# Two graph layers with experts: layer 1's adjacency product by pairs of panels in seven block products, and scores of three tiles in four by TensorE

## The chip, the cores and the metric

The kernel runs on one core of one Trainium2 chip. The core has a matrix engine (TensorE, PE in the profile; its weight loads are shown as PEld), a vector engine (VectorE, DVE), a scalar engine (ScalarE, ACT), a general engine (GpSimd, POOL) and a queue engine that issues transfers (SyncE, SP). They run side by side, each takes its own instructions in order, and they wait for one another by semaphores. The metric is the time of one execution on the device in microseconds (us), as the median over runs.

## The reference

Two layers work on 3327 nodes with 256 features each, in fp32. Each layer adds a graph step to `x`, and then a mixture of experts:

```
# layer 0
x = x + relu(adj @ (LN(x) @ W) + b)
x = x + moe0(LN(x))                        # 8 experts, 256 -> 1024 -> 256, best two of 8 per node
# layer 1
sim  = tanh(adj * adj);  filt = sim * (adj > 0)     # the 700 largest per row are kept
h2   = tanh(LN(x) @ W_proj + b_proj)
x = x + relu(filt @ (h2 @ W_gcn) + b_gcn)
t = LN(x)
x = x + t + sum over the best two experts of  p * (gelu(t @ w1[e] + b1[e]) @ w2[e] + b2[e])
```

`adj` is 3327 x 3327 with a few nonzero elements per row, but it is multiplied as a dense matrix. No row has more than 700 nonzero elements with these inputs, so the selection of the 700 largest leaves all of them; the kernel tests this and has another branch for the other case.

## The kernel before, in words

Nodes are padded to 3328, which is 26 tiles of 128 nodes, or 13 panels of 256 nodes. `x` and the features `s` (one row per node: `h2 @ W_gcn` in layer 1) stay in SBUF, with nodes on the partitions. The host hands over the transposed adjacency cut into 26 pieces: a panel (256 result nodes) by half of the source nodes (13 slices of 128). A piece is 1.7 MB. Six places in SBUF (`ring`, the constant `RING`) hold pieces; the tables `LOADS` and `ENDS`, made from `UNITS`, say in which order pieces are loaded and given up, and so which piece goes to which place.

Layer 0 aggregates its panels 2 to 11 by pairs (`pair` in `aggregate_first`). Two panels by two halves of the source nodes are a 2 x 2 block matrix, and the two halves of the source nodes by two halves of the features are another. The scheme of Strassen and Winograd gets their product from seven block products where the plain way has eight. It needs sums of blocks: four sums of whole pieces per pair (`add_pieces`, line 480, on VectorE, in place, each in four parts) and, once, four sums of feature blocks (`sum_features`, kept in `pad` as `half_sums`). There the features are the stationary operand and the piece, 256 columns wide, is the moving one, so that the results lie with features on the partitions (line 470), and a product with `W` turns them.

Layer 1's aggregation is `aggregate` (lines 430 to 450). For each panel it runs 52 matmuls (two halves, two result tiles, 13 slices): the piece gives the stationary 128 x 128 operand, `s[:, j, :]` with all 256 features is the moving one, and results lie with nodes on the partitions, as `x` does. Then `add_relu` (lines 403 and 404) adds bias, relu and residual. `filter_chunk` (lines 1656 to 1661) turns a loaded piece into `tanh(max(a, 0)^2)` in place: the maximum on VectorE, Square and Tanh on ScalarE. The first four pieces are filtered by `filter_behind` while the features are still being made.

`after1` (lines 1683 to 1695) does the routing behind each panel. It lists the tokens of the panel before (`list_tokens`: two small bf16 matmuls per tile, lines 770 and 771, give each token its place in the list of its expert, and GpSimd scatters each token twice, line 793). Then it normalizes the two tiles (`statistics`, then line 371 on VectorE) and scores them: `scores` (line 662) is eight multiply-and-sum instructions per tile on VectorE, one for each expert. The last panel's tiles are scored by TensorE instead (`by_features` turns the tiles by `transpose`, `scores_by_product` multiplies, line 672). `weights` picks the two best experts (`top_two`), takes the exponential on ScalarE (line 729) and makes the shares. GpSimd adds the normalized tokens to `x` (line 1690) and copies them for the second expert (line 765). At panel 9 `plan_early` makes, from the tokens of panels 0 to 8, a table of eight full blocks of 256 tokens, and at panels 10 and 11 the first four of these blocks, with their experts' weights, are loaded into free places of the ring.

After the last panel (`first_blocks`) the expert blocks run one after the other; the last panel's routing and the plan of all other blocks come between the first three of them.

The order of the instructions on each engine is made at build time. A scheduler walks through the program with a model of the times and takes, for each engine, the first instruction in program order that its model holds to be ready; the engine then keeps that order on the chip. `issue_after` and `behind` force an instruction behind another one on the same engine.

## Time and profile before

| | |
|---|---|
| median of 4 runs | 1202.94 us (1200.27 to 1203.8) |
| the profiled execution: its own time | 1199.63 us |
| the profiled execution: span from first to last instruction | 1197.8 us |
| mean granted TensorE clock | 0.987 |
| layer 1's aggregation | 750.5 to 1045.9 us of the span |
| in it: TensorE, VectorE, ScalarE, GpSimd busy | 295.4, 243.6, 154.9, 72.9 us |
| from there to the end | 151.9 us, TensorE busy 121.9 |

How to read the lines: a line of a view names the engine, the line of the kernel (L440), the operation, what is written and read (`ps_g<-s,ring`), the shapes, and how many instructions are merged (x104). In the views in order of time a line begins with start and duration in us. In brackets stands the idle time of the engine before the instruction, and what ended it. A matmul in fp32 leaves two records, and so does its weight load. Matmuls are pipelined: the duration of one is longer than the distance from one to the next, and the distance is what a series costs. A line can be that of a helper: L793 is every scatter, L480 every sum of pieces.

### The profile page before, as it was taken

To read this page: it belongs to the slowest core of one execution; us is meant where nothing else is said; L and a number is where in the kernel's file an instruction comes from. 1 tells how busy PE (TensorE), PEld (TensorE's weight loads), DVE (VectorE), ACT (ScalarE), POOL (GpSimd) and SP (SyncE) were. 2 spreads that over 40 slices of the span, in tenths; PEclk is the share of its full clock that TensorE was granted. 3 is DMA by queue.
4 is the path that set the end of the run, shared out by engine and by line. 5 is a ranking of instruction groups with operands and counts; after the bars stand their busy time and mean duration, and the time that the engine had idled before them with its cause. 6 is when DMAs were issued, how large, how long until landed. Compare 5 with 4: busy or idle time off the path is not lost. (4 is left out here: it accounts for less than half of the span.)

```text
span 1197.8 us, 19704 instructions
## 1 busy us (share of the span) xinstructions
PE 1156.5 (97%) x6217; PEld 1006.7 (84%) x6217; DVE 865.8 (72%) x3001; ACT 556.9 (46%) x1051; POOL 291.6 (24%) x367
## 2 busy tenths in 40 slices
PE   8999999999899999999999999999999999989983
PEld 7888888888688888898988888888888888877862
DVE  6798999988865555554545679299999998784464
ACT  5599566541224333434334346976546542033331
POOL 2111242143421112111111110022232232265442
PEclk9999999999999999999999999999999999999997
DMA  9895747634366555757565964245445442467697
GB/s 348 192 325 187 255 144 210 246 126 144 110 232 230 197 185 191 264 181 264 190 232 171 368 239 166 97 150 189 165 174 189 155 184 75 131 205 234 209 291 226
DMA packets 123185, 241.68 MB, mean 202 GB/s; under 512 B 24480, under 2 KB 93120, under 8 KB 116160
## 3 DMA queue, kind: packets, MB, share of 16 engines
q1 hardware_dynamic: 108656, 205.59, 51.7%
q0 software_dynamic: 11136, 31.60, 7.1%
q10 hardware_dynamic: 3280, 3.15, 0.8%
q8 instruction: 51, 0.84, 0.3%
q14 instruction: 62, 0.51, 0.1%
HBM read 203.98 MB, written 36.33 MB: 201 GB/s over the span
## 5 line engine op out<-in xcount | busy, mean ns | idle before, releaser
L440 PE MATMUL ps_g<-s,ring 128*128 128x256 f32 x1352 | 294.2, 380 | 0.0
L440 PEld LDWEIGHTS ps_g<-s,ring 128*128 128x128 f32 x1352 | 256.0, 190 | 34.4
L1234 ACT ACTIVATE pad<-ps_h,ring 128x256 f32<-128x256 f32 (+1 forms) x282 | 128.8, 458 | 296.7 <-issue 143.9
L1226 PE MATMUL ps_h<-pad,ring 128*128 128x256 f32 (+1 forms) x1184 | 254.5, 367 | 5.0 <-issue 2.6
L1226 PEld LDWEIGHTS ps_h<-pad,ring 128*128 128x128 f32 x1184 | 200.5, 190 | 47.9 <-ACT pad L1234 10.5
L662 DVE SCALAR_TENSOR_TENSOR rt_product<-xn,gate 128x256 f32<-128x256 f32 x400 | 194.8, 487 | 16.1 <-ACT xn L360 2.8
L793 POOL DMA_INDIRECT ys<-pad,index x114 | 116.4, 1021 | 369.6 <-DVE pad L1281 236.1
L793 POOL DMA_INDIRECT xlist<-xn,rt_idx x104 | 115.4, 1110 | 157.1 <-DVE ln_nw L347 60.8
L1495 ACT ACTIVATE sign<-ring,below 128x416 bf16<-128x416 f32 x208 | 133.4, 641 | 11.8 <-DMA ring<-in_adjT 5.9
L470 PE MATMUL ps_g<-ring,pad 128*128 128x256 f32 x520 | 115.0, 380 | 0.0
L470 PEld LDWEIGHTS ps_g<-ring,pad 128*128 128x128 f32 x520 | 98.5, 190 | 13.2
L1660 ACT ACTIVATE ring<-ring 128x3328 f32<-128x3328 f32 x22 | 65.4, 2978 | 87.3 <-DVE ring L1659 56.3
L1281 DVE SCALAR_TENSOR_TENSOR pad<-ps_y,ring,pad 128x128 f32<-128x128 f32 x176 | 59.2, 348 | 47.6 <-PE ps_y L1274 47.4
L470 PE MATMUL ps_g<-ring,s 128*128 128x256 f32 x390 | 89.6, 379 | 0.0
L470 PEld LDWEIGHTS ps_g<-ring,s 128*128 128x128 f32 x390 | 74.1, 190 | 10.1
L480 DVE TENSOR_TENSOR ring<-ring,ring 128x768 f32<-128x768 f32 (+1 forms) x80 | 79.6, 1013 | 0.0
L495 PE MATMUL ps_g<-ring,s 128*128 128x256 f32 x312 | 69.1, 380 | 3.5 <-ACT s L360 3.0
L495 PEld LDWEIGHTS ps_g<-ring,s 128*128 128x128 f32 x312 | 58.9, 190 | 12.7 <-ACT s L360 3.7
L1661 ACT ACTIVATE ring<-ring 128x3328 f32<-128x3328 f32 x22 | 65.4, 2978 | 0.6
L1265 DVE TENSOR_TENSOR xnT<-pad 128x512 f32<-128x512 f32 x22 | 15.2, 692 | 59.2 <-ACT pad L1234 59.2
L1323 PE MATMUL ps_y<-ring,pad 128*128 128x256 f32 x224 | 56.3, 399 | 0.0
L776 POOL COPY xn<-rt_w 128x4 f32<-128x4 f32 x26 | 4.8, 198 | 201.0 <-DVE rt_w L738 200.9
(240 smaller groups left out, 1587.7 us busy)
## 6 DMA issues: line engine op xcount, KB each, us to landing
ring<-in_adjT SPq DMA_DIRECT2D x50, 1664.0 KB
ring<-in_f_w1T SPq DMA_DIRECT2D x30, 1024.0 KB
ring<-in_f_w2T SPq DMA_DIRECT2D x30, 1024.0 KB
ring<-xlist SPq DMA_DIRECT2D x52, 258.0 KB
ring<-in_f_w SPq DMA_DIRECT2D x36, 256.0 KB
ring<-ys SPq DMA_DIRECT2D x12, 512.0 KB
ring<-in_f_b SPq DMA_DIRECT2D x34, 128.0 KB
xlist<-h2T SPq DMA_DIRECT2D x16, 257.0 KB
```

Source lines behind the costliest of these rows:

```text
L440: nc.tensor.matmul(ps[it], lhsT=chunks[k][:, c, ts(it, P)], rhs=s[:, j, :], start=(j == 0), stop=(j == NT - 1),)
L470: nc.tensor.matmul(ps, lhsT=b[:, c, :], rhs=a[:, c, :], start=(first and c == 0), stop=(c == CJ - 1), skip_group_check=not first,)
L480: nc.vector.tensor_tensor(out[:, part, :], out[:, part, :], other[:, part, :], ALU.add)
L495: nc.tensor.matmul(sums[pan][c], lhsT=s[:, j, ts(c, P)], rhs=piece(pan, j // CJ)[:, j % CJ, :], start=(j == 0), stop=(j == NT - 1),)
L662: nc.vector.scalar_tensor_tensor(product, xn, 1.0, gate[:, e, :], ALU.mult, ALU.mult, accum_out=sc[:, g, e : e + 1],)
L793: d = nc.gpsimd.indirect_dma_start(out=a[:, :], out_offset=bass.IndirectOffsetOnAxis(ap=index, axis=0), in_=rows_, in_offset=None,)
L1226: last_product[:] = [nc.tensor.matmul(ps, lhsT=w1[:, c, ts(hc, P)], rhs=xT[:, c, :], start=(c == 0), stop=(c == DC - 1),)]
L1234: nc.scalar.activation(hT[:, hc, :], ps, func, bias=bb1[:, hc : hc + 1])
L1281: last_y[:] = [nc.vector.scalar_tensor_tensor(part, ps, xb[:, g, WT : WT + 1], part, ALU.mult, ALU.add)]
L1495: nc.scalar.activation(sign, piece(pan, k)[:, :, ts(i, GROUP)], AF.Sign, bias=below, accum_out=positive[:, pan, i, k : k + 1],)
L1660: nc.scalar.activation(a, a, AF.Square)
L1661: nc.scalar.activation(a, a, AF.Tanh)
```

## The change

Layer 1's panels are cut into units: panel 0 alone, the pairs (1,2), (3,4), (5,6), (7,8) and (9,10), and panels 11 and 12 alone. A pair is done in seven block products with the same sums as in layer 0, but the piece stays the stationary operand and the half block of features (128 columns) is the moving one, so that results lie with nodes on the partitions. Each product is 13 slices by two result tiles; the PSUM results are copied by ScalarE into `g1` and `g2` or added to them by VectorE, and `add_sums` adds bias, relu and residual for a whole panel.

The routing of a unit is cut into named steps (`route1`), which run at fixed places within the next unit, as hooks within a product or between products. Normalization moves to ScalarE (`scaled`). Of the four tiles of a pair, three are scored by TensorE and one by VectorE where another pair follows, and two by each where panel 11 follows (`BY_PRODUCT`). Panel 0's two tiles are scored by TensorE, panel 11's two by VectorE. Of the four pieces that are filtered in a pair, two have their maximum taken by VectorE and two by a Relu on ScalarE. The passes of ScalarE over a piece are put between its other work (`run`, `passes`), each behind the last copy. `shares` moves from `weights` into `list_tokens`. The early plan is made from the same panels 0 to 8, but within the last product of the pair (9,10); the four early blocks are loaded as places come free from then on.

```diff
+BY_PRODUCT = {(1, 2): 2, (2, 2): 3, (2, 1): 2, (1, 1): 0}
 UNITS = (
     [(pan,) for pan in range(SIDE)] + [(pan, pan + 1) for pan in range(SIDE, NPAN - 1, 2)] + [(NPAN - 1,)],
-    [(pan,) for pan in range(NPAN)],
+    [(0,)] + [(pan, pan + 1) for pan in range(1, NPAN - 2, 2)] + [(NPAN - 2,), (NPAN - 1,)],
 )
...
-    def aggregate(b_sb, prepare, after):
...
+    def aggregate(b_sb, route, freed, turn, copied):
...
+        def filter_next(on_vector):
+            if not loaded_:
+                return
+            a = piece(*loaded_.pop(0)).rearrange("p c w -> p (c w)")
+            if on_vector:
+                with behind(normal):
+                    nc.vector.tensor_scalar(a, a, 0.0, None, ALU.max)
+            for f in ([] if on_vector else [AF.Relu]) + [AF.Square, AF.Tanh]:
+                passes.append((a, f))
+
+        def run(n):
+            for a, f in passes[0:n]:
+                with behind(copied):
+                    last_pass[:] = [nc.scalar.activation(a, a, f)]
+            del passes[0:n]
...
+        def multiply(ps, a, b, first=True, hooks=()):
+            hooks = dict(hooks)
+            ps = by_tile(ps)
+            for c in range(CJ):
+                for it in range(PW // P):
+                    nc.tensor.matmul(
+                        ps[:, it, :], lhsT=a[:, c, ts(it, P)], rhs=b[:, c, :],
+                        start=(first and c == 0 and it == 0), stop=(c == CJ - 1),
+                        skip_group_check=True,
+                    )
+                if c in hooks:
+                    hooks[c]()
...
+        def add_sums(pan, g):
+            x_t = x[:, pan * 2 : pan * 2 + 2, :]
+            nc.vector.tensor_tensor(g, g, b_tiles, ALU.add)
+            nc.vector.scalar_tensor_tensor(x_t, g, 0.0, x_t, ALU.max, ALU.add)
+
+        def pair(p1, p2, step, ps_x, ps_q, ps_b, ps_z):
+            a11, a12, a21, a22 = (piece(pan, k) for pan in (p1, p2) for k in range(NCHUNK))
+            b11, b21, b22 = half(0, 0), half(1, 0), half(1, 1)
+            t3, t2, t4, t1 = half_sums
+            run(len(passes))
+            multiply(ps_x, a11, b11)
+            (g1, (c11, c12)), (g2, (c21, c22)) = sums_of(), sums_of()
+            copy(c11, ps_x)
+            step("statistics")
+            with behind(last_shift):
+                add_pieces(a11, a21)
+            add_pieces(a21, a22)
+            filter_next(False)
+            run(2)
+            multiply(ps_q, a22, t4)
+            copy(c21, ps_q)
+            run(1)
+            filter_next(True)
+            step("normalized")
+            add_pieces(a22, a11)
+            run(1)
+            multiply(ps_b, a12, b21)
+            nc.vector.tensor_tensor(c11, c11, by_tile(ps_b), ALU.add)
+            add_pieces(a12, a22)
+            step("other scores")
+            turn_ = lambda: step("turned")
+            multiply(ps_z, a21, t1, hooks={2: turn_, 7: turn_})
+            run(1)
+            copy(c22, ps_z)
+            free(p2, 0)
+            score = lambda: step("scores")
+            multiply(ps_x, a22, t2, False, {2: score, 6: score})
+            step("weights")
+            copy(c12, ps_x)
+            free(p2, 1)
+            filter_next(False)
+            run(1)
+            step("exponentials")
+            run(2)
+            multiply(ps_z, a12, b22, False)
+            free(p1, 1)
+            nc.vector.tensor_tensor(c12, c12, by_tile(ps_z), ALU.add)
+            add_sums(p1, g1)
+            multiply(ps_x, a11, t3, False, {2: lambda: step("listed"), 8: lambda: step("planned")})
+            filter_next(True)
+            for part in (c21, c22):
+                nc.vector.scalar_tensor_tensor(
+                    part, part, -1.0, by_tile(ps_x), ALU.mult, ALU.subtract
+                )
+            add_sums(p2, g2)
+            free(p1, 0)
...
+                hooks = {
+                    0: lambda: step("statistics", "normalized"),
+                    2: lambda: step("other scores"),
+                    16: lambda: step("turned"),
+                    18: lambda: step("turned"),
+                    28: lambda: step("scores"),
+                    30: lambda: step("scores", "weights", "exponentials"),
+                    42: lambda: step("listed"),
+                    48: lambda: step("planned"),
+                }
+                if turn and u[0] == NPAN - 1:
+                    hooks[22] = turn
+                single(u[0], hooks, banks[0:2])
...
-        if group == "0":
-            w = shares(w, n)
+        w = shares(w, n)
...
-    def panels1(layer1, turn=False):
...
+    def route1(pans, by_product, ready, copied):
...
+        def normalize():
+            for at in range(0, n, 2):
+                xn = work.tile([P, 2, K, RW], F32, name="xn")
+                for g in range(2):
+                    copied.append(scaled(xn[:, g, 0, 0:D], t + at + g, at + g, q.rs, q.shift))
+                x_t = x[:, t + at : t + at + 2, :]
+                nc.gpsimd.tensor_tensor(x_t, x_t, xn[:, :, 0, 0:D], ALU.add)
+                q.xns.append(xn)
+            q.sc = work.tile([P, n, E], F32, name="rt_sc", bufs=2)
...
+        def turn_(i):
+            q.xnTs.append(turned_tiles(tiles_at(i), "xnT"))
+            copied.append(last_turned[0])
+
+        def score(i):
+            m = len(tiles_at(i))
+            scores_by_product(q.xnTs[i], m, f1_r_sb, q.sc[:, 2 * i : 2 * i + m, :])
+
+        def score_rest():
+            for g in range(by_product, n):
+                score_tile(q.xns[g // 2][:, g % 2, 0, 0:D], q.sc[:, g, :])
...
+        def plan_():
+            if pans[-1] + 1 == EARLY_PANS[1]:
+                plan_early(EARLY_PANS[1])
+            if pans[-1] + 1 >= EARLY_PANS[1]:
+                ready()
...
-        aggregate(gnn_b_sb, filter_chunk, panels1(layer1, True))
+        aggregate1(layer1, layer1.turn_first)
```

## The prediction

> **What bounds the kernel now.** I read the busy time by engine first, then the windows of layer 1's aggregation, then the matmuls by shape, then the instructions in order of time.
>
> ```profile
> PE 1156.5 (97%) x6217; PEld 1006.7 (84%) x6217; DVE 865.8 (72%) x3001; ACT 556.9 (46%) x1051; POOL 291.6 (24%) x367
> ```
> ```profile
> 750.50:1045.90 295.40, 295.40 (x1410) 259.24 (x1409) 243.63 (x924) 154.94 (x86) 72.86 (x91) 1.00 0.43 150
> 1045.90:1197.80 151.90, 121.87 (x624) 100.01 (x622) 86.99 (x331) 48.14 (x99) 67.56 (x69) 0.92 0.74 235
> ```
> The columns of a window are: length, then busy time of PE, PEld, DVE, ACT, POOL, then granted clock, DMA share, GB/s. The stage that is changed lasts from 750.5 to 1045.9 us, and TensorE has no gap in it at full clock (1.00). So only TensorE's own work, or a wait that is new to it, moves the end of this stage. What follows (151.9 us) hangs on the end of panel 12 in both kernels.
>
> ```profile
> 796.44 0.17 PE L770 MATMUL pr<-rt_both,before 128*128 128x8 bf16 x1
> ...
> 796.54 22.69 PE L440 MATMUL ps_g<-s,ring 128*128 128x256 f32 x104
> 819.07 0.17 PE L770 MATMUL pr<-rt_both,before 128*128 128x8 bf16 x1
> ```
> A panel lasts from one listing to the next: 819.07 - 796.44 = 22.63 us; four small listing matmuls take 0.10 of it, so 104 records of 256 columns take 22.53 us, 0.2166 us each. (An fp32 matmul leaves two records, so 52 matmuls are 104.)
>
> ```profile
> 402.25 0.97 PEld L1274 LDWEIGHTS ps_y<-gate,pad 128*128 128x128 f32 x8
> 403.14 0.97 PEld L1274 LDWEIGHTS ps_y<-ring,pad 128*128 128x128 f32 x8
> 404.03 1.87 PEld L1274 LDWEIGHTS ps_y<-gate,xnT 128*128 128x128 f32 x16
> 405.82 0.97 PEld L1274 LDWEIGHTS ps_y<-ring,h2T 128*128 128x128 f32 x8
> ```
> This is layer 0's expert in seven products: the shape that the change brings in (128 weights, 128 moving columns). From 402.25 to 405.82, 32 records: 0.1116 us each. The load's own duration is 0.192 us, but loads start 0.112 us apart, so the spacing and not the duration counts.
>
> ```profile
> 194.30:237.30 43.00, 43.00 (x212) 37.79 (x209) 40.28 (x134) 26.74 (x73) 12.57 (x14) 1.00 0.68 219
> ```
> One pair of panels in layer 0, already done in seven products: TensorE busy for all of 43.0 us although VectorE works for 40.28.
>
> **The change, part by part.**
>
> *Products.* Ten of thirteen panels go by pairs. Removed: 10 x 22.53 = 225.3 us. Added per pair: 7 products x 13 slices x 2 halves of the panel x 2 records = 364 records of 128 columns, x 0.1116 = 40.6 us; five pairs 203.1. Panels 0, 11 and 12 stay as they are. Saved: 22.2 us, all of it on the engine that sets the end. One eighth would be 28; six go because a record of half the columns costs 0.1116 instead of 0.1083.
>
> A rule stands against this. The Trainium skill (TensorE: Matmul & The Clock Gate, "LDWEIGHTS (loading the stationary operand)" and "The mechanism") prices a load at its columns over 1.2 GHz, 107 ns here, and says that loads overlap matmuls in flight only where the row group differs. With full 128-row loads that adds about 0.107 to each record; by this estimate a pair would take some 79 us and the change would lose about 170. The row above was taken with exactly these shapes and shows 0.1116 for load and matmul together, so the sum goes by the row.
>
> *Scores by TensorE.* Tiles scored so: two of panel 0, three of four in the pairs (1,2) to (7,8), two of (9,10): 2 + 12 + 2 = 16. A tile needs two transposes and four records of scores.
>
> ```profile
> 400.93 0.46 PEld L1172 LDWEIGHTS ptb<-ident,ring 128*128 128x128 f32 x4
> 401.35 0.97 PEld L1274 LDWEIGHTS ps_y<-ring,pad 128*128 128x128 f32 x8
> ...
> 1055.08 0.97 PEld L672 LDWEIGHTS pg<-f_r_sb,xnT 128*128 128x128 f32 x8 [0.21 <-ACT xnT L388]
> 1055.97 0.73 PEld L1226 LDWEIGHTS ps_h<-pad,ring 128*128 128x128 f32 x4
> ```
> Four transposes take 401.35 - 400.93 = 0.42, eight score records 0.89. A tile: 0.21 + 0.45 = 0.66 us, and 16 tiles 10.5 us, in the middle of TensorE's row. Nothing covers it there. The eight-column output does not help, since its loads are full.
>
> *VectorE per pair,* from layer 0's 40.3 us: three tiles fewer of scores (32 of them with their reads took 14.3 + 2.6, so -12.7); two filter passes (2 x 1.88 = +3.8; the other two pieces go to ScalarE); bias and relu on two panels as four instructions of 0.68 instead of eight of 0.42 (-0.7); the output sums nearly as before (+0.2); two score copies (+0.3); layer 0's bias on the scores goes (-0.2). Sum 31.0. To this comes GpSimd's x + xn, which layer 0 lacks:
>
> ```profile
> 849.06 2.06 DVE L662 SCALAR_TENSOR_TENSOR rt_product<-xn,gate 128x256 f32<-128x256 f32 x1
> ...
> 849.54 1.28 POOL L1690 TENSOR_TENSOR x<-x,xn 128x512 f32<-128x512 f32 x1
> ```
> A VectorE instruction of 0.42 took 2.06 while it ran. Two of these per pair: +2.6, so 33.6 of a pair's 42.9 us (40.6 + 2.0 for three tiles + 0.3 for eight listing records). VectorE does not become the bound by its sum.
>
> The sums of the weights (four instructions of 1.88) run once, in panel 0, in which VectorE was busy for 3 of 22.6 us: no cost.
>
> *ScalarE per pair:* Square and Tanh on four pieces and Relu on two, 10 x 2.98 = 29.8; four normalizations of 0.59; four PSUM copies of 0.37; two copies of turned tiles, 0.59 + 0.37; one Exp of 0.20: 34.9 of 42.9. No table load: the trace has four in all, and Relu, Identity, Exp, Square and Tanh alternate elsewhere without one.
>
> *Waits, walked through a pair,* t from its first product; products end near 5.8, 11.6, 17.4, 23.9 (with transposes), 30.9 (with scores), 36.7, 42.8. On VectorE the last pair's two sums, relu and residual end at 2.2, its statistics and shift, a chain of some 13 small steps of 0.2 each, at 6.3; the first two panel sums (3.98 each, from four parts of 1.21 and 0.95) at 14.3: product 4 starts at 17.4, slack 3.1. A filter pass (1.9), the third sum and the 2.6 of GpSimd give 22.8: product 5 starts at 23.9, slack 1.1. The fourth sum ends at 27.2 against 30.9. On ScalarE a Relu, Square and Tanh stand ahead of the normalizations, which end near 17.7; the first transposes come at 18.3, slack 0.6. Thus no stall by the rows, but two slacks near one microsecond. Bounds: 0 from layer 0's pair, which had none with more on VectorE; from above, every sum at its slowest part (1.23 x 4) and all 4.2 us of GpSimd's sums and copies falling on them: 6.3 + 3 x 4.9 + 1.9 + 4.2 = 27.1, product 5 waits 3.2 per pair, 16 in all. I take 0 in the pairs, as the nearest row does.
>
> *Panel 11* has the whole routing of pair (9,10) in 22.6 us with two tiles scored by VectorE (2 x 4.2), after the early plan (some 27 small steps, about 6 us, moved from panel 9's end to this pair's last product). Plan, sums and statistics reach to about 10, scores to 20, weights to 23, while the listing is written at 18. TensorE may wait there: between 0 and 5, taken as 1.5. The expert loads queue on SyncE behind the last pieces, not ahead, and wait for scatters that land near 10 us into panel 11; the first is used 20 us later: no cost.
>
> *Piece loads.* Two pieces issued together at 841.94 were through by 852, so one is there about 7 us after its issue; freed at 23.9 and 30.9, needed at 42.8 or later after two or three passes: hidden. The order of the first six pieces changes, and the first pair needs its fourth piece 11.6 us after panel 0, at 784.8; before, the sixth piece's Tanh ended near 785.2. 0 to 0.5, taken as 0.
>
> *After the stage:* panel 11's list is made inside panel 12 instead of behind it. That frees 5 us of GpSimd's queue, on which TensorE doesn't wait. 0.
>
> Sum: -22.2 + 10.5 + 1.5 = -10.2 us. The profiled execution took 1199.63 us (span 1197.8 and 1.8 around it) and would take 1189.4. The median of the runs shown, 1202.94, lies 3.3 above it, so the forecast is 1192.7.
>
> **Rivals.**
>
> 1. *Slower:* product 5 waits for the third panel sum in every pair. For it: VectorE's window is filled in layer 0 to 40.28 of 43.0, GpSimd's lock is real (2.06 for 0.42), slack is 1.1. Against it: layer 0's pair, busier, has no gap. It cancels the gain at 10.2 / 5 = 2.0 us per pair; at the upper bound of 3.2 it costs 16: 1208.7. The Trainium skill (SBUF — State Buffer, "SBUF: two separate sides") calls the shared port an exclusive lock when a VectorE instruction has two SBUF inputs, as the panel sums have. The row of 2.06 agrees; by the page too it is GpSimd's own time that VectorE can lose.
> 2. *Partial:* ScalarE's row runs late (normalizations behind three passes, a piece that lands late), and transposes or listings stand in TensorE's queue for about 1 us per pair, panel 11 for 5: +3.5 to +9, 1196 to 1202.
> 3. *Better:* transposes and scores slip into the gaps between products, or the products' loads overlap better than in short runs. With half of the 10.5 gone and no wait in panel 11: -17, 1186.
> 4. *The change doesn't do what it says:* a record of 128 columns costs the load's whole 0.192 in a long run. A pair would take 70 + 2.3 us, 135 more in all, 1338. The 56 records in a row at 0.112 speak against it; 1%.
>
> **How the numbers follow.** Forecast 66%, with its own range 1188 to 1198; partial 14%; slower 14%; better 5%; the last 1%. Runs of this kernel can tell about 0.2% (2.4 us) from no change. Below 1200.5: the forecast, the better case and half of the partial one, 78%; within 0.2%: 7%; above 1205.3: 15%. Range 1184 to 1207: down to a better case, up to half-way into the slower one.
>
> **What would show it.** Right: the pairs' matmuls 0.112 us apart and a pair in 43 us; the stage ends near 1036 instead of 1045.9; VectorE about 34 of 43 per pair. Wrong: idle TensorE before products 4 or 5 released by VectorE's panel sums, before transposes released by ScalarE's normalizations, or before panel 11's listing; a spacing above 0.12.

## The result, and the profile after

The changed kernel takes 1200.07 us (median of 52 runs, 1194.34 to 1207.89) beside 1201.37 us of the kernel before (78 runs). The ratio is 0.9985, with a 95% interval from 0.9977 to 0.9993: some 1.8 us less, which is within the 0.2% that I took as no change. The forecast was 1192.7 us. The profiled execution took 1199.55 us with a span of 1197.8 us, the same span as before.

The busy time by engine, after:

```profile
PE 1145.7 (96%) x7093; PEld 1022.3 (85%) x7093; DVE 851.6 (71%) x2667; ACT 603.5 (50%) x1110; POOL 313.0 (26%) x367
```

TensorE works 10.8 us less than before (1156.5), close to the sum of the terms *Products* and *Scores by TensorE* (-22.2 + 10.5 = -11.7). The work went, and the time stayed. The windows of the stage and of what follows, and then of the stage's units (the five pairs, panel 11, panel 12), show where; the columns are length, busy time of PE, PEld, DVE, ACT, POOL, then granted clock, DMA share, GB/s:

```profile
748.30:1044.60 296.30, 289.07 (x2287) 277.77 (x2286) 227.28 (x594) 202.16 (x145) 94.98 (x93) 0.99 0.44 154
1044.60:1197.80 153.20, 121.83 (x620) 100.12 (x618) 87.65 (x327) 48.02 (x99) 64.94 (x68) 0.92 0.71 226
```
```profile
771.60:813.76 42.16, 42.16 (x381) 42.14 (x380) 29.46 (x63) 36.19 (x20) 8.69 (x4) 1.00 0.45 162
813.76:856.69 42.93, 42.93 (x392) 42.92 (x391) 37.64 (x86) 33.78 (x22) 11.86 (x13) 1.00 0.49 174
856.69:899.62 42.93, 42.93 (x393) 42.92 (x391) 37.92 (x86) 33.14 (x22) 16.89 (x16) 1.00 0.52 184
899.62:944.23 44.61, 44.31 (x393) 43.36 (x392) 37.73 (x86) 33.16 (x22) 16.35 (x16) 1.00 0.51 178
944.23:988.66 44.43, 44.16 (x393) 43.46 (x392) 38.24 (x92) 33.37 (x22) 17.04 (x17) 1.00 0.40 140
988.66:1018.80 30.14, 23.47 (x114) 19.77 (x113) 20.61 (x95) 5.86 (x8) 12.05 (x14) 0.89 0.42 128
1018.80:1044.57 25.77, 25.77 (x129) 22.64 (x127) 18.37 (x80) 3.36 (x6) 12.07 (x16) 1.00 0.42 139
```

Before, TensorE had no gap in this stage; now the stage has 7.2 us of gaps (296.30 - 289.07) and a clock below 1.00. The second and third pair take 42.93 us, where the prediction said 42.9. The fourth and fifth take 1.7 and 1.5 us more. Panel 11 takes 30.14 us for 23.47 of work, part of it at a low clock. The stage as a whole takes 296.3 us where 285 were forecast. That it starts 2.4 us earlier than before (748.3 against 750.7) and is followed by 1.3 us more (153.2 against 151.9) makes the spans equal.

The products, in order of time (a line has the start, the duration, the operation and, after the x, the records that are merged):

```profile
813.76 5.97 PE L679 MATMUL ps_g<-s,ring 128*128 128x128 f32 x52
819.57 5.97 PE L679 MATMUL ps_g<-pad,ring 128*128 128x128 f32 x52
825.38 5.97 PE L679 MATMUL ps_g<-s,ring 128*128 128x128 f32 x52
```

From start to start 5.81 us for 52 records: 0.1117 us each, against 0.1116 forecast. The estimate that the prediction drew from the Trainium skill (TensorE: Matmul & The Clock Gate, "LDWEIGHTS (loading the stationary operand)" and "The mechanism"), by which each full 128-row load would add about 0.107 us, is not what this shape does on the chip. The second of these sections also names loads into a background weight buffer as pulled ahead of matmuls in flight; the prediction's estimate left that case out.

Panel 11, in order of time, is where it went wrong:

```profile
988.66 9.66 PE L753 MATMUL ps_g<-s,ring 128*128 128x256 f32 x44
1004.25 1.18 PE L388 MATMUL pt<-ident,xn 128*128 128x128 f32 x4 [5.93 <-ACT xn L361]
1005.23 4.22 PE L753 MATMUL ps_g<-s,ring 128*128 128x256 f32 x14
...
1017.98 0.18 PE L923 MATMUL pr<-rt_both,before 128*128 128x8 bf16 x1 [0.74 <-DVE rt_both L854]
```

The four transposes of pair (9,10)'s tokens wait 5.93 us for ScalarE's normalization, and stand in TensorE's queue ahead of panel 11's own matmuls. ScalarE has nothing to do before it; it waits for VectorE's `ln_shift`. And this is VectorE in the middle of the Newton steps (small steps that approximate one over a square root) that lead to it:

```profile
997.10 0.16 DVE L348 SCALAR_TENSOR_TENSOR ln_nw<-ln_guess 128x4 f32<-128x4 f32 x1
1002.89 0.17 DVE L1397 CAST index<-ring 128x2 int32<-128x2 f32 x1 [5.63 <-DMA ring<-xlist]
1002.97 0.15 DVE L349 TENSOR_TENSOR ln_nw<-ln_nw,ln_ve 128x4 f32<-128x4 f32 x1
```

An instruction that belongs to another stage stands between two steps of 0.2 us and waits 5.63 us for a transfer. It is in `place_of` (line 1397): the conversion of the first expert block's token numbers into whole numbers. The block's first work on TensorE comes 29 us later (1031.42), in panel 12. Its input is the block's tokens, and their load waits for the scatters of panels 7 and 8 (first the last scatter on GpSimd's queue, then the load on SyncE's):

```profile
997.31 0.97 POOL L945 DMA_INDIRECT xlist<-xn,rt_idx  x1 [0.30 <-issue]
```
```profile
1000.05 0.40 SPq L1288 DMA_DIRECT2D ring<-xlist  x1
```

In the kernel before, the same conversion stood later and waited for 0.81 us, and TensorE ran through:

```profile
1012.54 0.17 DVE L1245 CAST index<-ring 128x2 int32<-128x2 f32 x1 [0.81 <-DMA ring<-xlist]
```

The change moved the early plan from panel 9's end to the last product of pair (9,10), and the build-time scheduler puts each instruction where its model holds it to be ready; here the load came later than the place that it chose.

The wait has a second price. Windows of the same columns, around the gap:

```profile
998.00:1004.20 6.20, 0.32 (x2) 0.00 (x0) 0.55 (x4) 0.60 (x2) 0.66 (x3) 0.70 0.49 145
1004.20:1006.20 2.00, 1.95 (x7) 1.57 (x8) 0.99 (x1) 1.94 (x4) 1.43 (x2) 0.50 0.61 145
1006.20:1008.20 2.00, 2.00 (x8) 1.65 (x7) 1.93 (x5) 0.00 (x0) 2.00 (x3) 0.72 0.80 246
1008.20:1017.90 9.70, 9.04 (x46) 7.74 (x44) 9.23 (x40) 0.00 (x0) 0.75 (x1) 1.00 0.44 128
```

After the gap the granted clock is 0.50 for 2 us and 0.72 on average over 2 more. From the first of the four transposes to the next record it takes 0.98 us instead of 0.44, and the next 14 records take 4.05 us (1005.23 to 1009.28) instead of the 3.03 that 14 x 0.2166 gives: about 1.6 us together.

Panel 11 from the listing that opens it (983.80) to its own (1017.98) took 34.2 us. Its work is 40 records of 128 columns (4.5), 90 of 256 (19.5), four transposes (0.4), eight scores (0.8) and 0.2 of small matmuls: 25.4, counted by distances. The excess of 8.8 us is 5.93 + 0.74 of waits, about 1.6 of slow clock and some 0.5 around the two waits.

The rest of the loss is in the fourth and fifth pair. The weight loads of their second product, in order of time:

```profile
905.32 2.73 PEld L679 LDWEIGHTS ps_g<-pad,ring 128*128 128x128 f32 x22
908.36 0.52 PEld L679 LDWEIGHTS ps_g<-pad,ring 128*128 128x128 f32 x4 [0.31 <-issue]
909.11 1.28 PEld L679 LDWEIGHTS ps_g<-pad,ring 128*128 128x128 f32 x9 [0.22 <-issue]
910.59 0.52 PEld L679 LDWEIGHTS ps_g<-pad,ring 128*128 128x128 f32 x4 [0.20 <-issue]
```

They stop for 0.2 to 0.3 us every few records, and "issue" says that the profile shows nothing that they wait for. The product lasts 7.65 us instead of 5.97.

### The profile page after: what moved, and what is told of

The parts are those of the page before. It is cut to its first block, busy times and chain, and to the rows that moved or that the text cites. A ratio compares the mean times of both kernels' runs of the same rounds, so it can differ in the third digit from the quotient of the medians.

```text
span 1197.8 us, 21265 instructions
## 1 busy us (share of the span) xinstructions
PE 1145.7 (96%) x7093; PEld 1022.3 (85%) x7093; DVE 851.6 (71%) x2667; ACT 603.5 (50%) x1110; POOL 313.0 (26%) x367
## 5 line engine op out<-in xcount | busy, mean ns | idle before, releaser
L1378 PEld LDWEIGHTS ps_h<-pad,ring 128*128 128x128 f32 x1184 | 200.9, 190 | 48.3 <-ACT pad L1386 10.5
L459 DVE TENSOR_TENSOR ring<-ring,ring 128x768 f32<-128x768 f32 (+1 forms) x160 | 168.9, 1096 | 1.7 <-PE ps_g L679 1.7
L660 ACT ACTIVATE ring<-ring 128x3328 f32<-128x3328 f32 x54 | 160.1, 2979 | 0.8 <-DMA ring<-in_adjT 0.4
L945 POOL DMA_INDIRECT xlist<-xn,rt_idx x104 | 118.8, 1142 | 126.2 <-DVE rt_idx L934 51.7
L1647 ACT ACTIVATE sign<-ring,below 128x416 bf16<-128x416 f32 x208 | 133.4, 641 | 13.5 <-DMA ring<-in_adjT 7.5
L818 DVE SCALAR_TENSOR_TENSOR rt_product<-xn,gate 128x256 f32<-128x256 f32 x272 | 122.4, 450 | 15.6 <-ACT xn L361 6.0
L679 PE MATMUL ps_g<-pad,ring 128*128 128x128 f32 x1040 | 126.0, 277 | 0.6
L679 PEld LDWEIGHTS ps_g<-pad,ring 128*128 128x128 f32 x1040 | 120.1, 192 | 2.2 <-issue 1.7
L679 PE MATMUL ps_g<-s,ring 128*128 128x128 f32 x780 | 89.6, 275 | 0.0
L679 PEld LDWEIGHTS ps_g<-s,ring 128*128 128x128 f32 x780 | 88.4, 192 | 0.1
L753 PE MATMUL ps_g<-s,ring 128*128 128x256 f32 x312 | 70.0, 384 | 0.0
L753 PEld LDWEIGHTS ps_g<-s,ring 128*128 128x128 f32 x312 | 59.6, 193 | 8.0
```

The costliest lines, as they stand in the source:

```text
L459: nc.vector.tensor_tensor(out[:, part, :], out[:, part, :], other[:, part, :], ALU.add)
L660: last_pass[:] = [nc.scalar.activation(a, a, f)]
L679: nc.tensor.matmul(ps[:, it, :], lhsT=a[:, c, ts(it, P)], rhs=b[:, c, :], start=(first and c == 0 and it == 0), stop=(c == CJ - 1), skip_g ...
L753: nc.tensor.matmul(banks_[it], lhsT=piece(pan, k)[:, c, ts(it, P)], rhs=s[:, j, :], start=(j == 0), stop=(j == NT - 1),)
L818: nc.vector.scalar_tensor_tensor(product, xn, 1.0, gate[:, e, :], ALU.mult, ALU.mult, accum_out=sc[:, e : e + 1],)
L945: d = nc.gpsimd.indirect_dma_start(out=a[:, :], out_offset=bass.IndirectOffsetOnAxis(ap=index, axis=0), in_=rows_, in_offset=None,)
```

## The experiments

Kernels of one group ran on the same chip and share the runs of the kernel before there. Different groups ran on different chips or at different times, and the kernel before itself had medians from 1188.41 to 1207.75 us in them. So each is given as a ratio to the kernel before of its own group, with its 95% interval. "Stage" is the length of layer 1's aggregation in the trace, from its first matmul to the end of panel 12 (295.3 us before, 296.3 after).

| group | kernel | ratio to before | stage, us |
|---|---|---|---|
| 1 | `cast_behind` | 0.9942 [0.9921, 0.9963] | 287.9 |
| 1 | `cast_all_product` | 0.9935 [0.9910, 0.9960] | 289.8 |
| 1 | `cast_no_product` | 1.0120 [1.0093, 1.0146] | 305.0 |
| 1 | `before_scores` | 1.0208 [1.0174, 1.0243] | 318.2 |
| 2 | `after_again` | 0.9984 [0.9967, 1.0001] | 297.0 |
| 2 | `cast_behind_again` | 0.9936 [0.9916, 0.9955] | 291.2 |
| 2 | `cast_listing` | 0.9932 [0.9912, 0.9952] | 288.5 |
| 2 | `cast_two_listing` | 0.9948 [0.9931, 0.9964] | 292.9 |
| 3 | `after_third` | 1.0060 [1.0026, 1.0094] | 297.7 |
| 3 | `phase` | 1.0040 [1.0009, 1.0070] | 297.3 |
| 4 | `before_again` | 0.9987 [0.9967, 1.0007] | 295.2 |
| 4 | `cast_listing_again` | 0.9987 [0.9966, 1.0009] | 295.1 |
| 5 | `listing_control` | 0.9940 [0.9917, 0.9963] | 291.5 |
| 5 | `listing_shift80` | 0.9940 [0.9919, 0.9961] | 293.2 |
| 5 | `listing_shift160` | 0.9938 [0.9919, 0.9956] | 291.2 |

### The conversion at the head of VectorE's queue

One instruction of the changed kernel is moved: the conversion must stand behind the last bias-and-relu of panel 12. In the traces of the two kernels the order of the instructions on TensorE, VectorE, ScalarE and GpSimd differs in this one alone.

```diff
@@ add_relu
-        nc.vector.scalar_tensor_tensor(x_tile, t, 0.0, x_tile, ALU.max, ALU.add)
+        last_added[:] = [nc.vector.scalar_tensor_tensor(x_tile, t, 0.0, x_tile, ALU.max, ALU.add)]
@@ place_of
-            with behind(last_y):
+            with behind(last_y), behind(last_added if group == "1" else ()):
```

Expected of `cast_behind`:

> The changed kernel with one instruction moved: the conversion of the first expert block's token numbers (index<-ring), which in the changed kernel stands on VectorE in the middle of the statistics of pair (9,10), is forced behind the last bias-and-relu of panel 12; nothing else moves on any engine. Theory A (VectorE's queue was held by that one instruction, which waited 5.63 us for the load of the first expert block): the statistics end near 998 instead of 1003.4, the transposes of panel 11 wait about 1 us instead of 5.93, TensorE's clock is not halved behind the gap, and the program is 6 to 7 us shorter than the changed kernel, 0.993 of the kernel before. Rival B (VectorE is simply too full there, with the early plan, the sums and the statistics of four tiles in one stretch): the transposes wait as long as before, and the time changes by less than 1 us, 0.998 to 0.999. Rival C (the wait comes back before the listing of panel 11, which waits for the best two experts from VectorE): half of the gain, 0.996.

Panel 11 in its trace, in order of time:

```profile
983.72 9.66 PE L753 MATMUL ps_g<-s,ring 128*128 128x256 f32 x44
993.67 0.93 PE L388 MATMUL pt<-ident,xn 128*128 128x128 f32 x4 [0.30 <-ACT xn L361]
994.44 3.19 PE L753 MATMUL ps_g<-s,ring 128*128 128x256 f32 x14
...
1007.75 0.18 PE L923 MATMUL pr<-rt_both,before 128*128 128x8 bf16 x1 [2.32 <-DVE rt_both L854]
```

The transposes wait 0.30 us instead of 5.93, and the 14 records behind them run at full speed (3.19 us instead of 4.22). Panel 11 goes from listing to listing in 28.9 us instead of 34.2. Part of what is gained is given back at the listing, which now waits 2.32 us instead of 0.74. The ratio is 0.9942.

Since chips differ, the changed kernel and this one ran once more, side by side.

Expected of `after_again`:

> The changed kernel, unchanged, beside the kernel before on the same chip as the three below. Theory A (the held VectorE queue costs panel 11 some 5 us, and cast_behind gains by letting it go): 0.9985 of the kernel before, as measured over several chips, and cast_behind_again 4 to 5 us less than this run. Rival B (the chip of the first four runs was kinder to the changed kernel, and moving the conversion gained nothing): this run gives 0.994 to 0.995 itself, within 1 us of cast_behind_again.

Expected of `cast_behind_again`:

> The conversion of the first expert block's index behind panel 12's last bias and relu, once more, now beside the changed kernel itself. Theory A: 0.994 of the kernel before, and 0.9955 of the changed kernel (-5 us), with pairs of 42.9 us and transposes in panel 11 that wait under 0.5 us. Rival B: equal to after_again within 1 us.

The changed kernel gave 0.9984 again, with its transposes waiting 6.24 us and a stage of 297.0; the moved conversion gave 0.9936 and 291.2. By the medians (1198.83 and 1194.98 us) one instruction's place costs 3.9 us. The stages differ by 5.8, but not all of that is the instruction's: 5.4 us are gained in panel 11 (34.8 and 29.4 from listing to listing), 1.6 are lost in panel 12 to a clock that was halved behind the listing's wait of 2.23 us, and 2.1 are gaps in the fourth and fifth pair that this trace has less of (their part follows below). Theory A holds, and the rival that only the chip differed is out.

### What the scores by TensorE are worth

`before_scores` is the kernel before with the tiles of panels 0 to 11 scored by TensorE, and nothing else:

```diff
-        sc = scores(xns, n) if pan < NPAN - 1 else scores_by_product(by_features(xns[0], n), n, f1_r_sb)
+        sc = scores_by_product(by_features(xns[0], n), n, f1_r_sb)
```

Expected of `before_scores`:

> The kernel before, with one part of the change alone: the 24 tiles of panels 0 to 11 are scored by TensorE (two transposes, four score records a tile) where VectorE did it; panels stay single. Theory A (nothing covers these on a TensorE without gaps): 24 x 0.66 = 15.8 us longer, 1.013 of the kernel before. Rival (they slip between the products): less than 4 us longer, below 1.003.

It lost 23.5 us (1211.86 against 1188.41), 1.0 us for each of its 24 tiles and not 0.66, so the rival that they slip between the products is out. The waits of TensorE's weight loads in its aggregation (what was waited for, us in total, times, longest):

```profile
PEld pt L387 <- issue: 4.9, 9, 0.6
PEld pg L672 <- ACT xnT L388: 2.3, 11, 0.2
PEld pt L387 <- DVE xn L371: 1.7, 8, 0.5
PEld pt L387 <- PE ps_g L440: 1.6, 2, 1.0
```

These are 10.5 us of waits around transposes and scores. The tiles' own 15.8 and these waits make 26, a little more than was lost.

The other half, the products alone, is `cast_no_product`: the moved conversion, and no tile of panels 0 to 11 scored by TensorE. `cast_all_product` goes the other way, with every tile.

```diff
-BY_PRODUCT = {(1, 2): 2, (2, 2): 3, (2, 1): 2, (1, 1): 0}
+BY_PRODUCT = {(1, 2): 0, (2, 2): 0, (2, 1): 0, (1, 1): 0}     # cast_no_product
+BY_PRODUCT = {(1, 2): 2, (2, 2): 4, (2, 1): 4, (1, 1): 2}     # cast_all_product
```

Expected of `cast_no_product`:

> As cast_behind, but all tiles of layer 1's panels 0 to 11 are scored by VectorE, none by TensorE: the block products alone. If the prediction's sum for TensorE is right, its row gets 16 x 0.66 = 10.5 us shorter; but VectorE, busy 37.7 of 42.9 us in a pair of the changed kernel, gets three tiles more, 12.7 us, or 50.4 against 40.9 on TensorE. Theory A: VectorE becomes the bound of four pairs, each about 50 us, and panel 11 takes about 6 us more: some 35 us longer than cast_behind, near 1.022 of the kernel before. Rival (VectorE's work is hidden, its waits do not matter): 10 us shorter than cast_behind, 0.985.

Expected of `cast_all_product`:

> As cast_behind, but every tile of panels 0 to 11 is scored by TensorE: eight tiles more than in the change. Theory A (once the held queue is gone, TensorE's row alone sets the time): 8 x 0.66 = 5.3 us longer than cast_behind, 0.997 to 0.998 of the kernel before, less what is left of the wait before panel 11's listing, which goes since VectorE has 8 us less to do there. Rival B (VectorE is too full): as fast as cast_behind or faster, 0.99.

Without TensorE's scores the change loses: 1.0120. Windows of its second and third pair:

```profile
805.70:857.30 51.60, 46.35 (x418) 46.16 (x415) 48.86 (x127) 38.46 (x21) 11.36 (x10) 0.99 0.59 208
857.30:907.20 49.90, 47.00 (x398) 46.62 (x398) 47.12 (x138) 36.41 (x21) 18.90 (x16) 0.94 0.45 159
```

VectorE is busy for 47 to 49 us of these pairs, which TensorE would do in 41 (42.93 - 3 x 0.66), and TensorE stands at the listing, 18.6 us in five waits for `rt_both` in the whole stage. VectorE is the bound there. It took 19.4 us more than `cast_behind` (1202.19 against 1182.75), where Theory A had 35: two of the four pairs took about 50 us, the other two 47.9 and 46.7, and panels 11 and 12 took no more than there. With every tile by TensorE, the window of a pair, and below it the like pair of `cast_behind`:

```profile
851.30:894.80 43.50, 43.50 (x398) 43.50 (x396) 34.51 (x71) 33.27 (x22) 17.06 (x16) 1.00 0.52 182
```
```profile
850.08:893.00 42.92, 42.92 (x392) 42.91 (x390) 37.81 (x87) 33.14 (x22) 17.12 (x16) 1.00 0.53 185
```

From listing to listing such a pair takes 43.59 us (851.30 to 894.89) against 42.92: a tile costs TensorE 0.67 us and frees 3.3 us of VectorE. Its eight more tiles cost 8 x 0.67 = 5.4 us, and the waits of 0.30 and 2.32 us in panel 11 are gone. In the traces its stage is 1.8 us longer than that of `cast_behind`; the ratios, 0.9935 and 0.9942, don't tell the two apart. That TensorE's row sets the pairs is as Theory A has it, and the time is nearer to Rival B's.

### Where VectorE's tiles stand in the way

Expected of `cast_listing` (the moved conversion, all tiles of pair (9,10) and of panel 11 by TensorE, three of four in the other pairs: `(2, 2): 3, (2, 1): 4, (1, 1): 2`):

> With the conversion behind; all four tiles of pair (9,10) scored by TensorE instead of two, and both tiles of panel 11 instead of none. Theory A (in panel 11 VectorE's two scored tiles, 8.4 us, make the listing late by 2.7 us, and as much in panel 12): four tiles cost TensorE 4 x 0.6 = 2.4 us and the two waits of 2.7 and 3.1 go: -3.4 us against cast_behind_again, 0.991 of the kernel before. Rival B (the listing is late for another reason, such as the statistics): the waits stay and the tiles cost 2.4 us: 0.996.

Expected of `cast_two_listing` (the same with `(2, 2): 2`):

> As cast_listing, and two tiles instead of three in the pairs followed by a pair. TensorE's pair goes from 42.9 to 42.3 us, VectorE's from 37.9 to 41.3 us of it. Theory A (TensorE sets the pair until VectorE's sum reaches it): -0.6 x 4 = -2.4 us against cast_listing, 0.989 of the kernel before. Rival B (VectorE's chain from panel sums to the listing is already the bound at 41.3, as with no tile by TensorE, where pairs took 46.7 to 51.6): the listing waits 0.5 to 2 us per pair, so 0 to +6 us against cast_listing, 0.991 to 0.996.

In this trace of `cast_listing` neither the transposes nor the listing of panel 11 wait; it goes from 983.84 to 1010.15, 26.3 us, beside 34.8 in `after_again` and 29.4 in `cast_behind_again`. (In the four later traces of this kernel and its shifted variants the transposes do wait, for 1.2 to 2.0 us, and the panel takes 27.6 to 28.4.) The ratio is 0.9932. The gain on `cast_behind_again` is 2.7 us by the stages and 1.75 by the medians, where 3.4 was expected; the intervals are too wide to tell these apart. In `cast_two_listing` a pair takes 42.26 us with VectorE busy for 40.6 of it, as Theory A has it, and no listing waits but the fifth pair's, 0.6 us. But by the medians it was 3.5 us slower than `cast_listing` (1196.70 against 1193.23), by the stages 4.4, and the trace shows what neither theory named:

```profile
987.77 9.23 PE L753 MATMUL ps_g<-s,ring 128*128 128x256 f32 x42
1000.59 0.69 PE L388 MATMUL pt<-ident,xn 128*128 128x128 f32 x2 [3.58 <-issue]
```
```profile
989.89 1.89 DVE L653 TENSOR_SCALAR ring<-ring 128x3328 f32<-128x3328 f32 x1 [2.42 <-DMA ring<-in_adjT]
```

Here a filter pass of a late piece (line 653) stood at the head of VectorE's queue for 2.4 us, the early plan and the statistics came behind it, and the transposes waited 3.6 us. It looks like the same fault with another instruction, one that waits for a transfer and holds VectorE's chain behind it. But the same pass waits 0.99 us in `cast_listing` too, and VectorE came to it 5.1 us after the listing here and 2.3 us after it there; no run moved this pass alone, so its share in the 3.6 us is not shown.

### The gaps in product 2

These gaps without a wait were the open part. The first thought was that TensorE's instructions come late. The profile's table of DMA queues has two marked "instruction"; one of them (q8) moved 58 packets of together 0.95 MB, so 16 KB each, and 51 in the kernel before, which has fewer instructions on TensorE. By narrow windows one of these packets starts every 14 us or so of a pair and takes about 1 us, and in products 2 of pairs 2 to 5 one starts 12 to 14 us after the listing that opens the pair. The gaps lie at 13 to 17 us. `phase` makes the stream of TensorE 80 instructions longer at its start, in a gap:

```diff
-WARM = 54
+WARM = 94
```

Expected of `after_third` (the changed kernel again, as the neighbour):

> The changed kernel, unchanged, as the neighbour of the run below on the same chip. 0.9985 of the kernel before. In both traces so far the weight loads of the second product of the fourth and fifth pair have four, three and five gaps of 0.2 to 0.35 us in which nothing is waited for, 0.8 to 1.5 us per pair. If they belong to this kernel they come again in these two products; if they belong to the chip or the moment, they don't.

Expected of `phase`:

> The changed kernel with 94 instead of 54 warming matmuls at its start, which lie in a gap of 2.3 us there and cost no time; all later instructions of TensorE stand 80 places further on in its stream, everything else is as in after_third. Theory A (the gaps are late fetches of TensorE's instructions, and where they fall depends on the place in the stream): the gaps move to other records or vanish, by up to 3 us (0.9960 to 0.9985 of the kernel before). Theory B (the gaps come from what the DMA queues and SBUF do at that time): they stay in the second products of pairs four and five, at the same time after the first scatter, and the time is that of after_third within 1 us.

In `after_third` the gaps came again in product 2 of pairs 4 and 5, and one in pair 3. In `phase` pairs 4 and 5 had none, and pair 3 lost 3.5 us:

```profile
868.46 2.15 PEld L679 LDWEIGHTS ps_g<-pad,ring 128*128 128x128 f32 x17
871.78 0.30 PEld L679 LDWEIGHTS ps_g<-pad,ring 128*128 128x128 f32 x2 [1.16 <-issue]
872.53 0.19 PEld L679 LDWEIGHTS ps_g<-pad,ring 128*128 128x128 f32 x1 [0.46 <-issue]
```

That spoke for late instructions. So the shift was made on `cast_listing` too, and doubled, with a control beside them (and, before that, one more run of `cast_listing` beside the unchanged kernel before).

Expected of `before_again`:

> The kernel before, unchanged, run as if it were a change: 1.000, with an interval that shows how far two equal kernels can be told apart (0.2%). Its trace gives the length of layer 1's aggregation on the same chip as the run below: 295.3 us if the stage is as in the trace shown of before.

Expected of `cast_listing_again`:

> cast_listing on another occasion. Theory A (what it gains is in its own stage): the stage 8 to 10 us shorter than in before_again, 0.993 of the kernel before. Rival B (the chips differ in what they make of this kernel, as after_third's 1.006 suggests): 0.996 to 1.000, with the difference ahead of the stage, in code that the change leaves alone.

`cast_listing` gained 0.13% here, on the chip of its first run, and not 0.68%. The fifth pair took 47.9 us in it, with 5 us lost in product 2 alone: 3.3 us of gaps, and 1.7 because behind them the granted clock was halved for the last 28 records:

```profile
957.56 4.83 PEld L679 LDWEIGHTS ps_g<-pad,ring 128*128 128x128 f32 x28 [1.03 <-issue]
```
```profile
958.10:961.40 3.30, 3.30 (x18) 3.30 (x17) 3.30 (x4) 3.30 (x3) 2.26 (x2) 0.50 0.00 0
```

The fourth pair lost 1.2 us, and panel 11 took 27.7 us with transposes that waited 1.24. The stage was as long as that of `before_again` (295.1 and 295.2), so neither theory holds: the loss is within the stage. The profiled execution, 1198.85 us, was the fastest of twelve, so what the median of 1205.65 lost beyond it no trace shows. `before_again` gave 0.9987 with an interval that holds 1. So these gaps can cost from nothing to 5 us per pair and differ from run to run.

Expected of `listing_control`:

> cast_listing as the neighbour of the two runs below on the same chip: 0.993 to 0.999 of the kernel before, as its two runs gave. The weight loads of product 2 show gaps with no wait in pair 5 and at times in pair 4, beginning 12.5 to 15 us after the listing that opens the pair, where a packet of the queue marked instruction lands 12 to 14 us after that listing.

Expected of `listing_shift80`:

> cast_listing with 40 more warming matmuls at the start, so that TensorE's stream stands 80 instructions further on. Theory A (the gaps are TensorE waiting for a late block of its instructions; a block is 16 KB, 256 instructions, about 14.3 us of these products): the packets land 1 to 3 us earlier in the pair, pairs 4 and 5 lose their gaps (0 to 5 us), pair 3 can have some instead. Rival B (the gaps belong to the fourth and fifth pair, by what the DMA engines do there): pairs 4 and 5 keep them.

Expected of `listing_shift160` (80 matmuls of 8 columns behind the 54):

```diff
-    for _ in range(WARM):
-        nc.tensor.matmul(warm, lhsT=ones_sq, rhs=ones_sq, start=True, stop=True)
+    for n in [P] * WARM + [E] * 80:
+        nc.tensor.matmul(warm[:, 0:n], lhsT=ones_sq, rhs=ones_sq[:, 0:n], start=True, stop=True)
```

> cast_listing with 80 more warming matmuls of 8 columns, 160 instructions further on: a block ends 160 x 0.056 = 9 us earlier, 4 to 6 us after the listing. Theory A: the packets land there, as the scatters and the piece load only begin, and product 2 has no gap in any pair; gaps can come in product 1 if the piece load delays the packet. Between 0 and 5 us less than the control: 0.990 to 0.996 of the kernel before. Rival B: gaps in product 2 of pairs 4 and 5 as in the control.

The packets moved as foretold: they started 12.5 to 14.3 us after the listing in the control, 10.9 to 12.7 with the shift of 80, and at 5 to 6 and at 18 to 19 with that of 160. The shift of 80 again put the largest gaps into pair 3, but pair 5 kept some. But with the shift of 160, far from any packet, pair 4 has them where the control has them, 13.5 us after its listing (901.38):

```profile
914.85 0.52 PEld L679 LDWEIGHTS ps_g<-pad,ring 128*128 128x128 f32 x4 [0.20 <-issue]
915.61 1.17 PEld L679 LDWEIGHTS ps_g<-pad,ring 128*128 128x128 f32 x8 [0.24 <-issue]
917.10 0.52 PEld L679 LDWEIGHTS ps_g<-pad,ring 128*128 128x128 f32 x4 [0.32 <-issue]
```

What a pair takes from listing to listing beyond 42.93 us, in each trace:

| kernel | pair 3 | pair 4 | pair 5 |
|---|---|---|---|
| the profiled changed kernel | 0.0 | 1.7 | 1.4 |
| `after_again` | 0.0 | 1.5 | 1.7 |
| `after_third` | 0.6 | 1.4 | 1.9 |
| `phase` | 3.5 | 0.0 | 0.0 |
| `cast_behind` | 0.0 | 0.0 | 0.0 |
| `cast_behind_again` | 0.0 | 0.1 | 1.0 |
| `cast_listing` | 0.0 | 0.0 | 1.2 |
| `cast_listing_again` | 0.2 | 1.2 | 5.0 |
| `listing_control` | 0.0 | 1.0 | 1.8 |
| `listing_shift80` | 2.7 | 0.0 | 1.2 |
| `listing_shift160` | 0.0 | 1.5 | 1.1 |

So the theory of the late packet falls in the form that I gave it. What the traces show is that the gaps are always in product 2, 12 to 17 us after the listing, in pairs 3 to 5, while the eight scatters that follow the listing are on their way; that pair 2, with four scatters, has none in any trace; that the shift by 80 both times moved most of them into pair 3; and that `cast_behind` and `cast_all_product` in group 1 and `cast_two_listing` in group 2 had none in product 2. One thing more parts the pairs: in every pair of the table that lost 1.0 us or more, the last packet of these scatters starts 16.4 to 17.2 us after the listing, in every other 17.6 or later, and it is earliest (16.4, 16.6) where most was lost (3.5, 5.0). So the gaps and the scatters' transfers go together, and which makes which is not shown. The cause stays open. A run without the scatters of these pairs was not made: the lists then hold unwritten rows. All three kernels are at 0.994; the shift gains nothing.

## Why the prediction was wrong

*Products* and *Scores by TensorE* were right: 0.1117 us per record, pairs of 42.93 us against 42.9. A fourth tile cost 0.67 us (43.59 - 42.92) and a third as much (42.93 - 42.26), where the prediction had 0.66. TensorE's price of a tile holds in a pair but not in `before_scores`, where it was 1.0; I take that for the effect of the placement inside the products, but no run changed the placement alone.

*VectorE per pair* was too low, 33.6 us against 37.6 to 38.2. The removed tiles were priced by adding up durations, 4.2 us each; by `cast_all_product` against `cast_behind` a tile frees 2.9 to 3.3, because each short read lies within the end of the multiplication ahead of it (in panel 11 a multiplication lasts from 1009.27 to 1009.70 and its read from 1009.62 to 1009.70). Three tiles make about 3 us of the difference. The sums of pieces took 1.20 us each in such a pair instead of layer 0's 1.01, 16 of them 18.2 instead of 16.0; these 2.2 us are near the 2.6 that I had set for GpSimd's lock. Another 1.5 to 2 us stay unexplained. The error had no consequence at three tiles by TensorE. *ScalarE per pair* was right (33.1 to 33.8 against 34.9), and so was *Waits, walked through a pair* for the transposes and the panel sums: none waited.

*Panel 11* is the term that failed. It was set at 1.5 us, between 0 and 5; it measured 8.8. The step that broke is the sentence that the expert loads wait for scatters and "the first is used 20 us later: no cost". The load has a reader long before its use, the conversion, and the scheduler put that into VectorE's queue in the midst of the statistics. The moved early plan was followed on VectorE and on SyncE, but not to the instructions whose place depends on its time. Moving the conversion alone took 5.3 and 5.4 us off panel 11 in the traces of the two groups, and 3.9 us off the program where both ran side by side. Scoring the tiles of pair (9,10) and of panel 11 by TensorE brought the interval to 26.3 us in one trace, near the 25.8 of its own pure work (86 records of 256 columns, eight transposes, 16 scores), and to 27.6 to 28.4 in four others. The clock was not in the sum at all: about 1.6 us.

The gaps in product 2, 1.7 + 1.4 us between listings (44.61 and 44.32 against 42.93) in the profiled run, were in no term. Layer 0's pair, which the prediction took as the nearest row, shows none.

*Piece loads* cost nothing in the changed kernel; in `cast_two_listing` a late piece may have cost some. *After the stage* was set at 0 and measured +1.3 in the profiled pair of traces; I did not test it, and the start of the stage, in code that didn't change, differs more than that (746.2 to 756.7 us in the traces of the changed kernel and its variants).

In sum, against a forecast of -10.2 us the stage became 1.0 longer: 7.3 more in panel 11 (8.8 - 1.5), 3.1 in the two pairs, and 0.8 in small things. Of the rivals the partial one came nearest in its time, 1196 to 1202 with panel 11 for 5 us, but it had ScalarE late by its own passes; ScalarE stood idle for 11.6 us before the late normalization. So that 1200 lies where this rival had it is luck and not its mechanism.

What stays open besides the gaps: in group 3 the changed kernel was 0.6% slower than before, although its stage there is only 1.4 us longer than in the profiled run. Its stage started at 756.7 us, 8.4 later than in that run, but no trace of the kernel before was taken in that group, so I can't say whether the kernel or the moment made it.

No best version stands out. `cast_listing` has 0.9932, 0.9987 (with an interval that holds 1) and 0.9940 in three groups, and was 5.6 us below the changed kernel beside it (1193.23 against 1198.83); `cast_behind` has 0.9942 and 0.9936, `cast_all_product` 0.9935, and the intervals overlap.

## What to carry to other kernels

When a change moves a step that makes addresses or starts loads, look also for every short instruction that reads what is loaded: in an engine's fixed order such a reader can come to stand in the middle of a chain that has nothing to do with it, and a wait of that size can cost the bounding engine its clock as well. A saving on the bounding engine pays only as far as the engine next in line has room: here seven products without TensorE's scores were slower than eight. And gains of half a per cent should be measured beside the control on more than one occasion.

## What the runs showed of the hardware that I had not expected

After a wait of 5.9 us TensorE's granted clock was 0.50 for 2 us and 0.72 on average for 2 more; in `after_again`, after 6.2 us, it was 0.50 for 4 us; in `cast_two_listing`, after 3.6 us, 0.50 for 6 us. Waits of about 2.3 us went both ways: one of 2.32 us in `cast_behind` left the clock at 1.00, and one of 2.23 us in `cast_behind_again` was followed by 0.50 for 3.3 us:

```profile
1015.55 0.18 PE L923 MATMUL pr<-rt_both,before 128*128 128x8 bf16 x1 [2.23 <-DVE rt_both L854]
```
```profile
1015.80:1019.10 3.30, 3.30 (x12) 2.58 (x12) 1.59 (x13) 0.21 (x1) 0.33 (x3) 0.50 0.23 75
```

The gaps of 0.2 to 1.0 us in the fifth pair of `cast_listing_again` were followed by 0.50 as well. The Trainium skill (TensorE: Matmul & The Clock Gate, "Part 1: The HAM clock gate") has the clock fall to half after an idle window of about 3.4 us. The waits of 5.9, 6.2 and 3.6 us agree with that; the last two cases don't, since TensorE was never idle for 3.4 us in them, and here the measurement decides: a shorter wait can halve the clock, and does not always.

TensorE's weight loads can stall in steps of 0.2 to 1.2 us without a visible wait, always in the same product of a pair and not in every run; the pair lost 0 to 5 us by it, in the largest case 1.7 of them by the halved clock.
